# Constant products ahead of the node products at the two ends of a four-layer graph network

## The chip, the cores and the metric

The kernel runs on one core of a Trainium2 chip. The metric is the device time of one launch in microseconds, the median of several runs. A core has five engines that work side by side and each take their own instructions in order: PE (TensorE, matrix products into PSUM), DVE (VectorE), ACT (ScalarE), POOL (GpSimd) and SP (which here issues DMAs). PE has two rows in the profile: PE for the products and PEld for the loads of the stationary operand. TensorE's clock is throttled; the profile reports the share of full speed that was granted.

## The reference

128 graphs of 64 nodes with 128 features pass through four residual layers. `x` is (128, 64, 128), `adj` (128, 64, 64), weighted, about a quarter filled. Cut to what matters:

```python
# layer 0: continuous-filter convolution over all pairs i, j
h = relu(layernorm(x))
Wf = ssp(gauss(adj) @ W1.T + b1) @ W2.T + b2          # (B, N, N, 128)
y = einsum('bjf,bijf->bif', h @ Wa.T, Wf * adj * adj)
x = x + ssp(y @ Wd1.T + bd1) @ Wd2.T + bd2
# layer 1: hyperbolic attention
h = relu(layernorm(x))
p = proj(mobius_add(proj(mobius_matvec(W, h)), proj(expmap0(b_lin))))
loc = clip(logmap(p_i, p_j))                          # all pairs
att = sigmoid(silu(concat(self, loc) @ att_w1.T + att_b1) @ att_w2.T + att_b2)
s = sum_j(att * loc * adj)
s = silu(concat(self, s) @ mlp_w1.T + mlp_b1) @ mlp_w2.T + mlp_b2 + self
x = x + proj(expmap0(silu(logmap0(proj(expmap(s, p))))))
# layer 2: normalised graph convolution
h = relu(layernorm(x));  d = 1 / sqrt(adj.sum(2) + 1e-8)
x = x + (d_i * adj * d_j) @ h @ W + b
# layer 3: message passing
h = relu(layernorm(x));  deg = adj.sum(1)
m = where(deg > 0, (adj.T @ (h @ Ws)) / max(deg, 1) + h @ Wr, 0)
x = x + concat(h, m) @ W_upd
```

## The kernel before

The 128 graphs are cut into 16 groups of 8 (`GROUPS`). Two graphs share the 128 partitions, so a group is four pairs, and a tile of node features is 128 x 4 x 128. Nodes of each graph are sorted by degree, and only the slots of edges that exist are computed: the edge tiles of layers 0 and 1 run over a fixed pattern of slots instead of all pairs. Two constant bf16 tiles belong to that: `slot_k`, the slot numbers, and `bones_b`, a block matrix of ones, one 64 x 64 block for each graph of a pair.

Every stage of a group is a Python generator, a stream, that yields before each step: `load`, `order`, `layer0`, `layer1_nodes`, `layer1_edges`, `rest1`, `rest2`, and smaller streams that they start (`attention`, `rows`, `scores_of`, `heads` and others). The class `Weave` runs these steps in one fixed list, `ORDER`: an entry such as `layer1_nodes@-3` means "one step of that stream for the group three before the current turn". The list is run through once per turn, from turn -6 to turn 21, and groups that don't exist are left out. So in the middle five or six groups at different stages are interleaved on all engines; at the start only the first groups are there, and at the end only the last. The order on PE, DVE, ACT and POOL is exactly the order in which the steps emit instructions; only what stands behind the list (`enough`, the reading of its flag and the branch over a dense fallback) is placed by the scheduler. While a step runs, `w.now` is its stream, with `name` and `group`.

PSUM has two kinds of tiles: `big` (two banks, three buffers) for edge products, and `sm` (one bank, two buffers) for node products. `bank()` hands out the next `sm` bank; PE may write it when whoever read its previous content is done. The steps with a bank that the text speaks of, in their order for one group:

- `layer1_nodes`. It begins with the end of layer 0: the product of `y` with `wd1T` (L1739 to L1743), read by ACT; the product with `wd2T` (L1759), read by DVE. Then the transposes of the normed `h1` (L1243, tile n) read by ACT; the product with `wlinx` (L1794, in a `big`); the transposes of `hh` (L1243); the Gram products (L1932, L1934), read by ACT into `gr`; the product with `attT` (L1250, tile n), which ACT scales into `Sx`.
- `rest1`: the product with `bones` (L2192), read by DVE; after a `big` product (L1264) the hidden layer (L2210, L2211), read by ACT; the product with `m2T` (L1250), read by DVE (L2219).
- `rest2`: after a `big` product (L1264) the one with `w2g` (L1250); the ranks (L2348); the un-sorting product (L1257); the transposes of `h3` (L1243); three products with `wsu`, `wru` and `wupd` on the same transposed tile (L1250); the product with `adj` (L1257). DVE then forms the output (L2402, L2405, four L1307), and SP stores it (L2414).

Lines of helpers appear for whole classes of work: L1243 (`transposes`), L1250 (`pairs_mm`), L1257 (`graphs_mm`), L1264 (`by_graph`), L1217 (`evac`, a copy on ACT). The edge products L2089, L2107, L2111 and L2133 belong to layer 1, L1605, L1627, L1644 and L1673 to layer 0.

Of the kernel before, what the change touches and what calls it, by code (L numbers as in the profile page):

```python
# [11 lines left out]
F32 = mybir.dt.float32  # L12
# [9 lines left out]
GROUPS = B // (2 * NP)  # L22
P = 128
# [747 lines left out]


PE, DVE, ACT, POOL = "PE", "DVE", "ACT", "POOL"
ORDER = """
filter_of00@-2 duo02@-2 rest2@-5 rest2@-5 weights_of20@-2 layer1_nodes@-3 rest2@-5 neighbours00@-2
turned_from2@=0 weights2@=3 turned_from3@=-2 filter_of01@-2 layer1_nodes@-3 filter_of00@-2
# [171 lines left out]
def sparse_stack(ctx: ExitStack, tc: tile.TileContext, ins, out: bass.AP, flag):  # L948
# [10 lines left out]
    psm = ctx.enter_context(tc.tile_pool(name="s_psm", bufs=2, space=PSUM))  # L959

    w = Weave()
    V, S, G, T = nc.vector, nc.scalar, nc.gpsimd, nc.tensor
# [22 lines left out]
    bones_b, tri_b = (const.tile([P, P], BF, name=n) for n in ("bones_b", "tri_b"))  # L985
# [39 lines left out]
    slot_k = const.tile([P, SLOTS + SLOTS % 2], BF, name="slot_k")  # L1025
# [202 lines left out]
    def flat(t):  # L1228
        return t.rearrange("q p n -> q (p n)")

    def bank(n=P):
        return psm.tile([P, 512 // n, n], F32, name="sm", tag="sm")

    def big():
        return pbig.tile([P, 2, 512], F32, name="big", tag="big")
# [3 lines left out]
    def transposes(src):  # L1239

        pt = bank()
        for p in range(NP):
            T.transpose(pt[:, p, :], src[:, p, :], ident)  # L1243
        return pt

    def pairs_mm(lhsT, rhs):

        pt = bank()
        for p in range(NP):
            T.matmul(pt[:, p, :], lhsT=lhsT[:, p, :], rhs=rhs(p), start=True, stop=True)  # L1250
        return pt
# [179 lines left out]
    def order(g, st):  # L1431
# [13 lines left out]
        V.tensor_tensor(own, idb, bl(deg, N), ALU.mult)  # L1445
        yield on(PE, "sm")
        pt = bank(N)
        T.matmul(flat(pt)[:, 0:NP * N], lhsT=bones_b, rhs=flat(last_d), start=True, stop=False)
        T.matmul(flat(pt)[:, 0:NP * N], lhsT=bones_64, rhs=flat(own), start=False, stop=True)
# [971 lines left out]
    with tc.manual_schedule(engines={E.Activation, E.PE, E.DVE, E.Pool}):  # L2421
        for stream in (slots_ranks, weights0, weights1, weights2):
            w.add(stream(), group=-1)
        for g in range(GROUPS):
            st = {}
            for stage in (load, order, layer0, layer1_nodes, layer1_edges, rest1, rest2):
                w.add(stage(g, st), group=g)
        w.run(ORDER, GROUPS)
    assert not w.streams
# [37 lines left out]
```

## Time and profile before

| what | value |
|---|---|
| median of 3 runs | 1784.91 us (1784.58 to 1786.87) |
| the profiled execution | 1786.2 us |
| its span, first to last instruction | 1784.4 us |
| mean granted TensorE clock | 0.941 |
| PE busy | 1580.3 us (89%), 10487 products |
| DVE busy | 1537.2 us (86%) |
| ACT busy | 1507.6 us (84%) |
| POOL busy | 407.2 us (23%) |
| DMA, queue 1 | 52.19 MB, 12.2% of 16 engines |
| chain that ended last | ACT 42%, PE 36%, DVE 13%, issue 4%, POOL 3%, DMA 2% |

All times below are microseconds from the start of the span. The chain that ended last is followed back from the last instruction: at each step to what released it, or to the instruction ahead of it on its engine. "Issue" in it is time in which an engine waited for nothing that the profile shows. In lists of instructions, brackets hold the idle time of the engine ahead of the instruction, and what ended it. Matmuls are pipelined and their ends are modelled, so the length of a group of products includes a tail that overlaps what follows; the distance of starts tells what one costs in a row. An fp32 product of 128 x 512 appears as two records, a bf16 one as one.

### The profile page before, as it was taken

How to read it: one execution, taken by the hardware profiler on the slowest of the kernel's cores; microseconds unless marked ns; L12 is line 12 of the kernel's file. 1: busy time of each engine (PE TensorE's matmuls, PEld its weight loads, DVE VectorE, ACT ScalarE, POOL GpSimd, SP SyncE). 2: the span in 40 equal slices, each digit the busy share in tenths (PEclk: the TensorE clock that was granted, in tenths of full speed). 3: DMA queues.
4: the chain of work that ended last, by engine and by line, in shares of the span. 5: the costliest groups of instructions: out<-in, count | busy, mean ns of one | idle time of the engine just before them, and what ended most of it. 6: DMA issues, size and time to landing. Idle time of an engine off the chain costs nothing.

```text
span 1784.4 us, 30686 instructions
## 1 busy us (share of the span) xinstructions
PE 1580.3 (89%) x10487; PEld 873.9 (49%) x10487; DVE 1537.2 (86%) x4826; ACT 1507.6 (84%) x2816; POOL 407.2 (23%) x701
## 2 busy tenths in 40 slices
PE   3959899998989899898989899898989999897853
PEld 2424444545545455455545454554545555454442
DVE  5559799999999999999999999999999999887843
ACT  2858798989899898989899898989999898986632
POOL 2010113122221413223121312222141322312121
PEclk9989999999999999999999999999999999997875
DMA  2000202011110202011020201111020201102110
GB/s 62 6 1 7 57 7 52 13 38 30 28 46 16 58 7 56 18 34 34 16 58 12 62 7 43 24 27 46 16 58 1 57 11 30 34 15 50 42 29 8
DMA packets 57174, 54.24 MB, mean 30 GB/s; under 512 B 13616, under 2 KB 40624, under 8 KB 57008
## 3 DMA queue, kind: packets, MB, share of 16 engines
q1 hardware_dynamic: 57008, 52.19, 12.2%
q8 instruction: 85, 1.39, 0.3%
q14 instruction: 81, 0.66, 0.1%
HBM read 7.61 MB, written 4.19 MB: 7 GB/s over the span
## 4 chain that ended last, share of the span: by engine, by line
ACT 42%; PE 36%; DVE 13%; issue 4%; POOL 3%; DMA 2%; SPq 1%; DVEq 0%; ACTq 0%
PE big L2107 6%; ACT ex L1634 6%; PE big L1644 5%; PE big L2089 4%; PE sm L1250 4%; ACT ex L1637 4%; ACT ra L1679 4%; PE big L2111 3%; ACT e L1613 3%; ACT e L1610 3%; ACT L923 3%; PE sm L2133 2%; ACT n L1297 2%; ACT ex L2116 2%; ACT va L1594 2%
## 5 line engine op out<-in xcount | busy, mean ns | idle before, releaser
L1644 PE MATMUL big<-ex,w2T 128*128 128x512 f32 (+1 forms) x768 | 300.6, 521 | 12.6 <-ACT ex L1634 5.5
L1649 DVE SCALAR_TENSOR_TENSOR ex<-big,c_L_gnn_b,ra 128x1024 f32<-128x1024 f32 (+1 forms) x160 | 198.4, 1240 | 50.2 <-PE big L1644 49.3
L1627 PE MATMUL big<-e,w1T 64*128 64x512 f32 (+1 forms) x768 | 185.7, 576 | 11.3 <-ACT e L1613 9.1
L1644 PEld LDWEIGHTS big<-ex,w2T 128*128 128x128 f32 x768 | 131.4, 190 | 127.9 <-issue 71.3
L2116 ACT ACTIVATE ex<-big,c_L_gnn_att_b 128x1024 f32<-128x1024 f32 (+1 forms) x160 | 168.0, 1080 | 17.7 <-PE big L2111 17.4
L2107 PE MATMUL big<-va,U 64*128 64x512 f32 (+1 forms) x768 | 175.1, 531 | 7.9 <-DVE va L2092 6.8
L1634 ACT ACTIVATE ex<-big,c_L_gnn_b 128x1024 f32<-128x1024 f32 (+1 forms) x160 | 175.2, 1095 | 3.1 <-PE big L1627 1.6
L1673 PE MATMUL big<-va,a 64*128 64x512 f32 (+1 forms) x768 | 169.7, 540 | 2.2 <-ACT va L1594 1.0
L2111 PE MATMUL big<-slot_r,Sx 64*128 64x512 f32 (+1 forms) x768 | 166.0, 506 | 0.0
L1637 ACT ACTIVATE ex<-ex 128x1024 f32<-128x1024 f32 (+1 forms) x160 | 165.8, 1049 | 0.0
L1679 ACT ACTIVATE ra<-big 128x1024 f32<-128x1024 f32 (+1 forms) x160 | 159.5, 1008 | 5.5 <-PE big L1673 5.5
L1408 DVE TENSOR_TENSOR ex<-ex 128x512 f32<-128x512 f32 (+1 forms) x256 | 141.0, 551 | 1.0
L2072 DVE COPY_PREDICATED att<-oh,th 128x256 f32<-128x256 uint16 x256 | 110.4, 444 | 17.1 <-DMA th<-row 15.7
L2227 POOL TENSOR_TENSOR w<-w,hh 128x512 f32<-128x512 f32 x16 | 22.1, 1383 | 444.5 <-DVE w L2219 431.0
L923 ACT ACT_TABLE_LOAD x92 | 118.0, 1283 | 2.2 <-PEq L2455 0.7
L2089 PE MATMUL big<-oh,pqs 64*64 64x512 bf16 (+1 forms) x1152 | 115.0, 337 | 0.0
L2092 DVE COPY_PREDICATED va<-slot_r,big 128x1024 f32<-128x1024 uint32 (+1 forms) x96 | 103.1, 1075 | 12.9 <-PE big L2089 12.9
L1627 PEld LDWEIGHTS big<-e,w1T 64*128 64x128 f32 x768 | 66.7, 199 | 78.6 <-issue 23.1
L2111 PEld LDWEIGHTS big<-slot_r,Sx 64*128 64x128 f32 x768 | 73.9, 187 | 60.4 <-issue 60.4
L2133 PE MATMUL sm<-ex,aw2b 128*32 128x512 f32 (+1 forms) x640 | 89.3, 589 | 14.4 <-ACT ex L2116 14.4
L1673 PEld LDWEIGHTS big<-va,a 64*128 64x128 f32 x768 | 69.7, 193 | 62.0 <-issue 36.2
L1264 PE MATMUL big<-adjT,v 64*128 64x64 f32 x256 | 30.8, 402 | 71.7 <-ACT v L1292 71.7
(571 smaller groups left out, 3682.0 us busy)
## 6 DMA issues: line engine op xcount, KB each, us to landing
th<-row SPq DMA_DIRECT2D x128, 256.0 KB, 3.5
th<-row SPq DMA_DIRECT2D x64, 104.0 KB, 2.3
x<-in_x_dram SPq DMA_DIRECT2D x16, 256.0 KB, 2.8
out_dram<-v SPq DMA_DIRECT2D x16, 256.0 KB, 2.3
adj<-in_adj_dram SPq DMA_DIRECT2D x16, 128.0 KB, 2.3
e<-in_L_gnn_att_w_dram SPq DMA_DIRECT2D x2, 64.0 KB, 4.3
bR<-in_L_gnn_mlp_w_dram SPq DMA_DIRECT2D x2, 64.0 KB, 3.4
wupd<-in_L_gnn_W_upd_dram SPq DMA_DIRECT2D x1, 128.0 KB, 3.7
```

What stands on the lines that cost most here:

```text
L923: self.scalar.preload_act_table_set({"log": "natural_log_exp_and_others", "silu": "silu_and_others"}[table])
L1627: T.matmul(dst, lhsT=w1T[HALF[h], :], rhs=e[HALF[h], b, 0:W], start=True, stop=True)
L1634: act(ex[:, :, 0:wide], pre[:, :, 0:wide], AF.Exp, bias=b1)
L1637: act(ex[:, :, 0:wide], ex[:, :, 0:wide], AF.Ln, bias=1.0)
L1644: T.matmul(wf[:, b, cols], lhsT=w2T, rhs=ex[:, b if c < 2 else b ^ j, cols], start=True, stop=True)
L1649: V.scalar_tensor_tensor(two.rearrange("q (j r) -> q j r", j=2), wf[:, :, 0:wide], b2s, ra[:, :, 0:wide], ALU.add, ALU.mult)
L1673: T.matmul(nb[:, b, at * W:at * W + W], lhsT=rf[rows, p + j, :], rhs=factors[0][rows, k + j, :], start=True, stop=True)
L1679: act(ra[:, :, 0:wide], nb[:, :, 0:wide], AF.Copy)
L2089: T.matmul(rk[h, k, 0:W], lhsT=pqs[h, s, p, :], rhs=oh[h, p, at:at + W], start=s == 0, stop=s == 2)
L2107: T.matmul(pre[:, b, col], lhsT=U[h, p + k, :], rhs=coefs[h, k, :], start=True, stop=False)
L2111: T.matmul(pre[:, b, col], lhsT=Sx[s][h, p + k, :], rhs=slot_r[h, at:at + W], start=False, stop=s == 1)
L2116: act(a[:, :, 0:wide], pre[:, :, 0:wide], AF.Silu, bias=ab1)
```

## The change

`bank()` learns which stream it works for. If that is `layer1_nodes` of group 0 or of the last group, or `rest1` or `rest2` of the last group, it writes four bf16 products of the constants `bones_b` and `slot_k[:, 0:512]` into the whole new bank ahead of the node product that asked for it. Their results are never read: the node product starts the bank anew. Steps of nested streams (`attention`, `heads`, `order` and the like) have other names and stay as they are, and so do the `big` tiles.

```diff
 PE, DVE, ACT, POOL = "PE", "DVE", "ACT", "POOL"
+KEPT_BUSY = {("layer1_nodes", 0), ("layer1_nodes", GROUPS - 1), ("rest1", GROUPS - 1), ("rest2", GROUPS - 1)}
...
     def bank(n=P):
-        return psm.tile([P, 512 // n, n], F32, name="sm", tag="sm")
+        pt = psm.tile([P, 512 // n, n], F32, name="sm", tag="sm")
+        if w.now and (w.now.name, w.now.group) in KEPT_BUSY:
+            for _ in range(4):
+                T.matmul(flat(pt), lhsT=bones_b, rhs=slot_k[:, 0:512], start=True, stop=True)
+        return pt
```

In the changed kernel's instruction lists this is 92 products and 92 weight loads more on PE, in 23 places: six in `layer1_nodes` of group 0, six in that of group 15, three in `rest1` and eight in `rest2` of group 15. The order on ACT and POOL is the same as before. Behind the hand-written list, the copy of the flag from PSUM (L1566) stands behind the four L1307 of the last group on DVE instead of ahead of them, and SP issues the last store ahead of its load of the flag instead of behind it. Every line of the kernel below the edit is five further down.

## The prediction

> **What bounds the kernel now.** I read the page first: how full the engines are and where the clock drops.
>
> ```profile
> span 1784.4 us, 30686 instructions
> ...
> PE   3959899998989899898989899898989999897853
> ...
> PEclk9989999999999999999999999999999999997875
> ```
>
> In the middle PE, DVE and ACT all stand at nine tenths and the TensorE clock (PEclk) is nearly full. Only at the two ends, where one group is alone, do both sag: mean clock 0.941. Next I took the chain of waits near the last group's node chain, because a product that is put into PE's queue costs time only where PE is on that chain.
>
> ```profile
> 1603.81 1.41 PE big L2089 x12
> 1605.22 1.05 PE sm L1739 x2
> 1606.28 0.86 PE sm L1740 x2
> ...
> 1612.97 0.86 PE big L2107 x4
> 1613.83 0.46 PE big L2111 x4
> 1614.29 1.98 PE sm L1759 x16
> 1616.27 1.00 PE sm L2133 x8
> ...
> 1623.67 0.21 PE big L2111 x4
> 1623.88 0.60 PE sm L1243 x4
> 1624.51 0.59 ACT n L1217
> ```
>
> Columns: start, length, engine, tile, line, count. From 1599 to 1619 the chain is PE alone, each piece starting where the last ends: whatever is inserted here moves the end. Then the timeline of PE in rest2 of the last group, whose brackets give the idle time ahead of each product:
>
> ```profile
> 1754.65 1.97 PE L1264 MATMUL big<-adjT,v 64*128 64x64 f32 x16 [22.43 <-ACT v L1292]
> 1757.31 2.08 PE L1250 MATMUL sm<-w2g,a 128*128 128x128 f32 x8 [0.68 <-ACT a L1217]
> 1761.01 0.39 PE L2348 MATMUL sm<-r,bones_b 128*128 128x256 bf16 x1 [1.62 <-DVE r L2345]
> 1761.98 1.97 PE L1257 MATMUL sm<-v,r 64*64 64x128 f32 x16 [0.58 <-DVE r L2350]
> 1768.05 1.63 PE L1243 MATMUL sm<-ident,v 128*128 128x128 f32 x4 [4.09 <-ACT v L1292]
> 1770.35 2.07 PE L1250 MATMUL sm<-wsu,a 128*128 128x128 f32 x8 [0.68 <-ACT a L1217]
> 1772.21 1.91 PE L1250 MATMUL sm<-wru,a 128*128 128x128 f32 x8
> ```
>
> Four constant products fit free of charge only into brackets longer than themselves. Last, the clock itself. In microsecond windows it changes at 1704.9, 1718.5, 1722.0, 1728.8, 1735.7, 1776.5: steps of a multiple of 3.41 us. So I cut the tail on that grid (length, PE busy, others, clock, DMA):
>
> ```profile
> 1718.40:1721.80 3.40, 1.31 (x4) 0.55 (x4) 0.41 (x3) 2.67 (x6) 1.02 (x1) 0.99 0.01 2
> 1756.00:1759.40 3.40, 2.71 (x14) 2.22 (x14) 0.00 (x0) 0.59 (x1) 1.11 (x1) 0.50 0.00 0
> 1769.60:1773.00 3.40, 2.73 (x13) 2.65 (x13) 0.00 (x0) 1.13 (x2) 0.00 (x0) 0.50 0.00 0
> 1773.00:1776.50 3.50, 3.50 (x22) 3.27 (x22) 0.57 (x1) 1.19 (x5) 0.00 (x0) 0.50 0.00 0
> ```
>
> 2.7 of 3.4 us busy did not lift the half clock (it stays 0.50 after 1759.4); 3.5 of 3.5 did (1.00 from 1776.5). A slice at full clock with 1.31 busy lost it. Over the whole trace, full clock survived slices down to 47% busy.
>
> **The change, priced.** It removes and moves nothing in the emitted order ahead of the last lines; it adds 23 bursts of four bf16 128x512 products with a weight load each: 6 in layer1_nodes of group 0, 6 + 3 + 8 in layer1_nodes, rest1 and rest2 of group 15. The profile has no such row. At full clock: twelve L2089 products (64-row halves, in pairs, with their own weight loads) take 1.41 us, so 0.235 for 512 columns and 0.94 for four; L1448 and L1449 (256 columns) start 0.11 apart, so 0.88. I take **0.9**. At half clock: 24 records of L1250 take 5.49 (0.229 each) against 16 of L1759 in 1.98 (0.124), a ratio of 1.85: 1.67, or twice 0.9: 1.8. I take **1.75**. A burst waits for its bank alone, as its product did before, so it starts when PE is done with what is ahead; what is queued behind it is all later PE work.
>
> Group 0. At L1739, PE comes straight from L1250 (99.81 for 2.07) and ACT waits for the result (L1747 at 105.36): +0.9 (1.75 if it all falls in the half clock before 104). At L1759 (idle 1.30 before), at L1243 of n (4.62) and of hh (1.66) the idle time swallows it: 0; without that cover each would cost 0.9. At L1932 there is no gap, ACT's copy of gr starts 0.17 after PE and DVE has 0.25 to spare: +0.7 (0 to 0.9). At the attT product at 163.38, DVE's next eviction L1649 starts 0.76 after PE is done: +0.2 (0 to 0.9). Together 1.8. Since the chain runs on without a break, I let this shift last to the end.
>
> Group 15, layer1_nodes. L1739, L1759 and L1243 of n stand in the PE stretch shown: 3 x 0.9 = 2.7 (2.6 to 2.8). L1243 of hh follows L1264 (1647.27 for 2.08) with no gap, and ACT's copy at 1650.41 is next on the chain; half clock until about there: +1.3 (0.9 to 1.75). L1932, idle 0.68 before: 0.9 - 0.68 = +0.2 (to 1.07). The attT product at 1666.79 follows wupd without gap; DVE's L2040 has 0.1 to spare: +0.8 (to 0.9). Sum 5.0.
>
> rest1. At L2192 (idle 3.01) nothing; uncovered it would be 1.75. At L2210, straight after wupd: 0.9, less 0.4 because L2210 and L2211, 2.15 on the chain (half clock until 1728.8), would then run whole at full clock: the L2210/L2211 of the group before start 0.86 apart, so 1.72. Net +0.5 (0.2 to 1.3). At m2T (idle 0.17 before) 0.9 - 0.17 = +0.75, as DVE's L2219 waits for it. Sum 1.25.
>
> rest2, where the clock could pay back. Ahead of w2g: 1.75 cold against 0.68 idle, +1.07. But L1264, this burst, w2g and the next burst are now 7.5 us without a gap, so a whole slice fills, and the clock rises inside w2g: -0.5. Burst two (0.9) fits into 1.62; L2348 saves 0.1; burst three costs 0.9 - 0.58 = +0.3; L1257 goes from 1.97 to the 1.09 of its row at 1730.05: -0.9. Burst four fits into 4.09, transposes save 0.15 (1.63 to 1.48, their row at 1720.32). They fill 1.3 of a slice as at 1718.4, so the clock falls again: burst five 1.75 - 0.68 = +1.07. Bursts six to eight have no gap: 3 x 0.9 = +2.7; by then a slice is full, one earlier than before, so wru and wupd save 0.85 each (8 x 0.229 against 8 x 0.124), -1.7, and the adj product 0.3. Sum **+1.5**. Where the slices fall is open: shifting the grid through one period moves the sum between +0.4 and +2.7.
>
> A rule speaks on the fall. The Trainium skill, "TensorE: Matmul & The Clock Gate", Part 1, has the clock halved after an idle window of about 3.4 us. This trace halves it after slices 38% to 47% busy. By the page the clock would hold through the transposes and this part would be about -1.0, the total 1791.6; I go by the slices.
>
> Last lines: the flag's copy (L1566) moves behind the four L1307, and the branches that close the program wait for it; the final output DMA is issued ahead of SP's flag load instead of behind it. 1.1 us later on that path, of which SP's own path (DMA at 1778.77, branch 1779.20) hides most: +0.3 (0 to 0.5). Clock gained elsewhere, as n's transposes in group 0 (1.08 to 0.66) and wsu of group 14: -0.6 (0 to -1.8).
>
> Sum: 1.8 + 5.0 + 1.25 + 1.5 + 0.3 - 0.6 = 9.25. The profiled execution took 1786.2 (span 1784.4 and 1.8 around it) and would take 1795.5; it lies 1.3 above the median 1784.91, so the median should be **1794**. All lower ends together give +5, all upper ones +15.
>
> **Rivals.** *The clock is held up.* Bursts at half clock count for more than my slices say and keep the tail warm from 1645 on. For: the clock rose at 1718.5 on a slice not quite full. Against: 80% busy was not enough in four slices. Price: on the chain in half-clock stretches lie L1257 and L1264 of 1645 (4.0), L1243 and wsu to wupd of 1659 (7.1), L1257 of 1714 (2.0), wsu to L2210 of 1722 (6.8) and rest2 (15.0). At full clock by the rows above (1.09 for each L1257 and L1264, 0.124 a record for the rest) these 34.9 are 20.4: 14.5 back. The bursts, all warm, cost 11.8: net -2.7, 1782.2, not slower. It decides once more than 11.8 is won back; the bursts stand near only half of those stretches.
>
> *The shift is absorbed.* Bursts in the full stretches (group 0 and the first three of group 15, 4.5) vanish in pieces that the chain calls "issue" (2.23 at 103.12, 0.64 at 1627.68) and in the th DMA landings; hh, L1932 and attT too (2.3). Left: 2.45, 1787.4. Against: around 1605 PE idles nowhere.
>
> *The clock gets worse.* Bursts shift the work so that slices stay unfilled: against the sum, rest2 2.7 for 1.5 (+1.2), the burst of L1739 in group 0 cold (+0.85), hh and L1932 cold (+1.3), L2210 at its upper end (+0.8), attT cold (+0.85), no gain elsewhere (+0.6): 9.25 + 5.6 = 14.85, 1799.8. For: each burst then outlasts its bracket. Against: a gapless run longer than 6.8 us always holds a whole slice.
>
> **How the numbers follow.** Forecast 0.72, absorbed 0.12, worse 0.08, held up 0.08. The range 1788 to 1798 holds most of the forecast's own spread (1790 to 1800 with every end at once) and reaches down to the absorbed case; what it leaves out is the held-up case, most of the worse one and part of the absorbed. Less than 0.2% (3.6 us) can't be told from no change. Faster needs the held-up case with still less paid for bursts: half of it, 0.04. Within: the other half and most of the absorbed, 0.14. Slower: 0.82.
>
> **What would show it.** On the chain, new L1236-type pieces of 0.9 before L1739, L1759 and n's L1243 of group 15; idle brackets gone before wsu and w2g; full clock from about 1760 to 1770 (shifted) in rest2, half again at wsu. PE busy rises by about 20 us. I am wrong if the chain jumps over the bursts near 1605, or if the clock in rest2 stays full after the transposes.

## The result, and the profile after

| | kernel before | changed kernel |
|---|---|---|
| median (lowest to highest, runs) | 1784.91 us (1784.58 to 1786.87, 5) | 1793.49 us (1793.09 to 1795.09, 5) |
| ratio of the times, 95% interval | | 1.0045 [1.0034, 1.0055] |
| profiled execution: span | 1784.4 us | 1793.0 us |
| mean granted TensorE clock | 0.941 | 0.947 |

The change costs 8.6 us. A median of 1794 had been forecast, in a range of 1788 to 1798. A second set of its runs, taken beside three of the experiments, gave 1795.20 (1.0057 [1.0043, 1.0071]).

The page of the changed kernel:

```profile
span 1793.0 us, 30869 instructions
...
PE 1597.6 (89%) x10579; PEld 879.5 (49%) x10579; DVE 1538.0 (86%) x4826; ACT 1507.5 (84%) x2816; POOL 405.2 (23%) x701
...
PE   3969899998989899998989899898989899896854
...
PEclk9989999999999999999999999999999999998876
```

PE is busy 17.3 us more. The mean clock of this pair rose by 0.006, and in the page only its last four digits moved (7875 before, 8876 now). Over all runs it is 0.940 to 0.947 for the changed kernel and 0.937 to 0.945 for the unchanged one, so little changed. The constant products did not hold the clock up: between 1600 and 1780 half clock lasted 92.3 us before and 78.5 us now (81.7 in a second profile of the changed kernel).

The chain of waits at the same place as before (start, length, engine, tile, line, count; all lines are five further down, and L1236 is the burst):

```profile
1605.41 1.41 PE big L2094 x12
1606.83 0.97 PE sm L1236 x4
1607.80 0.86 PE sm L1744 x2
1608.65 0.86 PE sm L1745 x2
...
1616.65 0.97 PE sm L1236 x4
1617.62 1.78 PE sm L1764 x16
...
1627.01 0.97 PE sm L1236 x4
1627.98 0.45 PE sm L1248 x4
```

Each burst is a piece of the chain, as forecast. But a burst adds less than its 0.97: the product behind it is shorter than it was (0.86 for 1.05, 1.78 for 1.98, 0.45 for 0.60). So 0.15 to 0.2 us that belonged to that product alone now lies inside the burst; why, the traces do not show. The starts of what follows moved by 0.77, 0.76 and 0.82.

The same stretch of rest2 of the last group, on PE's timeline (brackets: idle time ahead, and what ended it):

```profile
1760.53 1.97 PE L1269 MATMUL big<-adjT,v 64*128 64x64 f32 x16 [22.44 <-ACT v L1297]
1762.43 1.89 PE L1236 MATMUL sm<-slot_k,bones_b 128*128 128x512 bf16 x4
1764.11 1.92 PE L1255 MATMUL sm<-w2g,a 128*128 128x128 f32 x8
1765.82 1.17 PE L1236 MATMUL sm<-slot_k,bones_b 128*128 128x512 bf16 x4
1767.65 0.27 PE L2353 MATMUL sm<-r,bones_b 128*128 128x256 bf16 x1 [0.66 <-DVE r L2350]
...
1768.71 1.09 PE L1262 MATMUL sm<-v,r 64*64 64x128 f32 x16
...
1773.90 1.63 PE L1248 MATMUL sm<-ident,v 128*128 128x128 f32 x4 [3.13 <-ACT v L1297]
1775.32 1.91 PE L1236 MATMUL sm<-slot_k,bones_b 128*128 128x512 bf16 x4
1777.03 1.92 PE L1255 MATMUL sm<-wsu,a 128*128 128x128 f32 x8
```

The brackets before w2g and wsu are gone, as forecast. The un-sorting product (L1262, L1257 before) takes 1.09 instead of 1.97, as it would at full clock; the transposes' bracket shrank from 4.09 to 3.13. Cut on the clock's steps (length, busy time of PE, PE's weight loads, DVE, ACT and POOL with counts, granted clock, DMA):

```profile
1759.30:1762.70 3.40, 2.17 (x17) 1.92 (x18) 0.16 (x1) 1.80 (x5) 1.36 (x3) 0.50 0.00 0
1762.70:1766.10 3.40, 3.40 (x13) 2.44 (x12) 0.00 (x0) 0.43 (x1) 0.28 (x1) 0.50 0.00 0
1766.10:1769.50 3.40, 2.74 (x23) 1.47 (x23) 1.94 (x6) 0.00 (x0) 0.00 (x0) 1.00 0.00 0
1769.50:1772.90 3.40, 1.27 (x10) 0.37 (x6) 1.62 (x12) 0.59 (x1) 1.06 (x2) 1.00 0.00 0
1772.90:1776.40 3.50, 2.50 (x7) 1.21 (x8) 0.16 (x1) 2.23 (x5) 0.16 (x1) 0.50 0.00 0
1776.40:1779.80 3.40, 3.40 (x13) 2.43 (x12) 0.00 (x0) 0.59 (x1) 0.00 (x0) 0.51 0.00 0
```

The full slice from 1762.7 lifted the clock at 1766.1, when the product with w2g had just ended. The slice with 1.27 busy dropped it again at 1772.9, so the transposes at 1773.90 already ran at half clock (1.63, as before). The next full slice, from 1776.4, lifted it once more at 1779.8.

Where the 8.6 us lie can be read from how much later the same instruction starts than before. The table sets the prediction's terms beside two profiled executions of the changed kernel; the second is that of e12_whole_again, below.

| term | forecast | first profile | second profile |
|---|---|---|---|
| what group 0 leaves (at 1603.7) | 1.8 | 1.60 | 1.31 |
| layer1_nodes of group 15 (to L2192) | 5.0 | 3.27 | 3.82 |
| rest1 (to m2T) | 1.25 | 1.09 | 1.08 |
| rest2 (to the first output operation) | 1.5 | 1.27 | 1.37 |
| last lines (to the end of the span) | 0.3 | 1.4 | 1.7 |
| clock gained elsewhere | -0.6 | in the rows above | in the rows above |
| sum | 9.25 | 8.6 | 9.2 |

The first row can't be put down to group 0: the profiles of seven kernels below without a burst there (e2, e3, e5, e6, e8, e9 and e10) stand at -2.05 to +1.72 us at the same place, from one execution to the next. And the rows of rest2 and of the last lines share a gain. With the flag's copy behind them, the output operations no longer stand behind it, and the first of them starts 1.14 us after the start of the last node product, the one with adj; with the copy ahead it is 1.52 to 1.69 (all at full clock). Without this, the row of rest2 would be about 0.4 to 0.55 higher, and that of the last lines as much lower.

### The profile page after: what moved, and what is told of

Same layout as the page of the kernel before. It is cut to its first block, busy times and chain, and to the rows that moved or that the text cites. A ratio compares the mean times of both kernels' runs of the same rounds, so it can differ in the third digit from the quotient of the medians.

```text
span 1793.0 us, 30869 instructions
## 1 busy us (share of the span) xinstructions
PE 1597.6 (89%) x10579; PEld 879.5 (49%) x10579; DVE 1538.0 (86%) x4826; ACT 1507.5 (84%) x2816; POOL 405.2 (23%) x701
## 4 chain that ended last, share of the span: by engine, by line
ACT 44%; PE 36%; DVE 11%; issue 4%; POOL 3%; DMA 1%; SPq 1%; DVEq 0%; ACTq 0%
PE big L2112 6%; ACT ex L1639 6%; PE big L1649 4%; PE big L2094 4%; ACT ex L1642 4%; ACT ra L1684 4%; PE sm L1255 4%; ACT e L1618 3%; PE big L2116 3%; ACT L924 3%; ACT e L1615 3%; PE sm L2138 2%; ACT ex L2121 2%; ACT n L1302 2%; ACT va L1599 2%
## 6 DMA issues: line engine op xcount, KB each, us to landing
th<-row SPq DMA_DIRECT2D x64, 104.0 KB, 2.3
```

## The experiments

Each kernel's time is compared with runs of the unchanged kernel on the same chip. Besides the ratio, the difference of the means is given, with a 95% interval from resampling the runs; single runs of one kernel lie up to 5 us apart, so about 1 us is the least that five to eleven runs can tell.

**The change in three parts.** The edit is the set of streams alone:

```diff
-KEPT_BUSY = {("layer1_nodes", 0), ("layer1_nodes", GROUPS - 1), ("rest1", GROUPS - 1), ("rest2", GROUPS - 1)}
+KEPT_BUSY = {("layer1_nodes", 0)}                               # e1_start
+KEPT_BUSY = {("layer1_nodes", GROUPS - 1)}                      # e2_nodes15
+KEPT_BUSY = {("rest1", GROUPS - 1), ("rest2", GROUPS - 1)}      # e3_rests15
```

> Only the six bursts in layer1_nodes of group 0 are left. Theory (a shift set early lasts to the end, since the chain of waits has no break): +1.45 us, the shift that the changed kernel's trace shows from 180 us on. Rival (the full middle of the kernel absorbs it in its short idle pieces): within 0.5 us of the kernel before.

> Only the six bursts in layer1_nodes of group 15. Theory (bursts in the PE-full stretch and behind it cost their own length where PE has no gap): 3 x 0.8 for L1739, L1759 and the transposes of n, 0.5 for hh and the Gram product, 0.35 for attT: +3.2 us. The prediction's terms were 2.7 + 1.5 + 0.8 = +5.0. Rival (absorbed in DMA landings and pieces called issue): under +1 us.

> Only the eleven bursts in rest1 and rest2 of group 15; the flag's copy stands behind the four output operations on DVE as in the changed kernel. Theory: rest1 +1.1, rest2 +1.35, the flag and the branches behind it +1.4: +3.85 us, with the clock rising inside the product with w2g and falling again after the transposes. Rival (the bursts hold the clock up and pay back): at most +1 us. Where the slices of 3.41 us fall is open: 1 us either way.

| kernel | median (runs) | ratio | difference of means |
|---|---|---|---|
| e1_start | 1785.17 (11) | 1.0002 [0.9993, 1.0011] | +0.3 [-0.5, 1.2] |
| e2_nodes15 | 1788.93 (11) | 1.0025 [1.0015, 1.0034] | +3.9 [3.2, 4.7] |
| e3_rests15 | 1789.07 (7) | 1.0022 [1.0011, 1.0033] | +3.5 [2.1, 4.9] |

The parts add up to 7.7 us. The whole is 8.7 by its means in the first set of runs and 10.2 in the second. With an interval of 0.8 to 1.4 us either way on each part, that shows no effect between them, and doesn't rule out one of 1 to 2 us. The node chain of group 15 costs less than the 5.0 of the prediction. The start alone costs nothing that could be told, though its trace shows a shift of 1.25 us at 200 us and 0.61 at 1603.7; in that profile the rest of the shift melted at the clock's edges in the tail (0.20 left at 1667.9, 0.03 at 1754.7), which came 0.3 us earlier than in the profile before while the work came later.

**Bursts in places that should be covered.** Counts per bank take the place of the set; here three places in layer1_nodes of group 0 (L1764, n, hh), the first bank of rest1 and banks two and four of rest2 have their four products, and no others:

```diff
+BURSTS = {("layer1_nodes", 0): (0, 4, 4, 4, 0, 0), ("rest1", GROUPS - 1): (4, 0, 0),
+          ("rest2", GROUPS - 1): (0, 4, 0, 4, 0, 0, 0, 0)}
...
+    calls = {}
...
-        if w.now and (w.now.name, w.now.group) in KEPT_BUSY:
-            for _ in range(4):
+        if w.now:
+            key = w.now.name, w.now.group
+            calls[key] = calls.get(key, -1) + 1
+            for _ in range(dict(enumerate(BURSTS.get(key, ()))).get(calls[key], 0)):
```

> Seven bursts alone, those that stand in idle brackets longer than 1.2 us: the product with wd2T and the transposes of n and of hh in group 0; the product with bones in rest1, and the ranks, the un-sorting product being left out, and the transposes of h3 in rest2 of group 15 (six places in all: three, one, two). Theory (a covered burst costs nothing): 0 us, down to -0.5 if the transposes of n stay at full clock. Rival (any burst delays what follows it on PE, covered or not, by 0.1 to 0.9): +0.6 to +5 us.

Measured: 1785.75 (11 runs), ratio 1.0000 [0.9991, 1.0009], difference +0.4 [-0.3, 1.1]. Six of the 23 bursts are free within about a microsecond. One of them is not covered as the prediction read it: at the product with wd2T of group 0 the burst itself waits for 1.29 us, as the product did, and starts only behind that idle time. What takes up its 0.86 us is a second idle piece, of 0.83 us, that the kernel before has inside that product.

**Does an early shift last?** e1_start left two answers: a shift from group 0 is given back on the way, or it was only too small to be seen. One long burst at L1744 of group 0 settles that:

```diff
+BURSTS = {("layer1_nodes", 0): (24,)}
```

> One burst of 24 products ahead of L1739 in group 0, nothing else: some 6.4 us of PE time, of which about 5 us are left behind L1743. Theory of the prediction (an early shift lasts to the end): +4.5 to +5.5 us. Rival A (a fixed slack of about 1 us in the middle takes it up, as six bursts of four brought +0.3 instead of +1.45): +3.5 to +4.5. Rival B (each rise of the clock at its fixed slice edge halves a shift, so little of any shift is left after fifteen groups): under +2 us.

Measured: 1791.29 (5 runs), 1.0042 [1.0029, 1.0056], +7.3 [6.4, 8.3]. In the trace the shift is 5.2 us behind the burst, 5.3 to 6.1 through the middle and 5.3 at 1754. A shift of 5 us set early lasts. The time rose by more than the trace's shift and by more than any theory had said; the profiled execution (span +4.5) is the fastest of its kernel, and the rest stays unexplained.

**The last burst and the flag's copy.** In the changed kernel the flag's copy stands behind the four output operations. e5 and e11 take the last burst out, which puts the copy ahead again; e10 adds one single product to the unchanged kernel, which puts it behind; e12 is the whole change once more, beside e10 and e11.

```diff
+BURSTS = {("rest1", GROUPS - 1): (4,) * 3, ("rest2", GROUPS - 1): (4,) * 7}    # e5_rests15_no_last
+BURSTS = {("rest2", GROUPS - 1): (0, 0, 0, 0, 0, 0, 0, 1)}                     # e10_last_one
+BURSTS = {("layer1_nodes", 0): (4,) * 6, ("layer1_nodes", GROUPS - 1): (4,) * 6,    # e11_all_but_last
+          ("rest1", GROUPS - 1): (4,) * 3, ("rest2", GROUPS - 1): (4,) * 7}
```

> As the kernel with the bursts of rest1 and rest2 alone, without the last burst (ahead of the product with adj); with it gone the flag's copy stands ahead of the four output operations again, as in the kernel before. Theory (the flag behind the output costs 1.4 us at the end, the burst 0.86): 2.2 us less than that kernel, +1.3 against the kernel before; the last output operation to the end of the span shrinks from 8.2 us (first output operation at 1784.85, end at 1793.0) to 6.8. Rival (the flag's place is hidden behind SP's own path): 0.9 to 1.2 us less.

> The unchanged kernel with one single constant product, ahead of the very last node product (the one with adj in rest2 of the last group). That is enough to put the flag's copy behind the four output operations and SP's last store ahead of its load of the flag, as in the changed kernel. The product itself costs 0.23 us. Theory from the traces so far (first output operation to the end of the span 6.6 to 7.0 us with the copy ahead, 7.7 and 8.2 behind): 0.9 to 1.4 for the order, +1.1 to +1.6 in all, and 7.7 us or more from the first output operation to the end. Prediction's term (SP's own path hides most of it, +0.3, at most 0.5): +0.5 in all, 7.3 us at most.

> The changed kernel without its last burst (ahead of the product with adj in rest2): 22 bursts, and the flag's copy is ahead of the output operations again. Against the whole change run beside it: theory, 0.9 for the burst and 0.9 to 1.4 for the order of the last lines, -1.8 to -2.3 us; prediction's terms, 0.9 + 0.3 = -1.2 us. The order of the last lines shows in the trace as 6.6 to 7.0 us from the first output operation to the end instead of 8.2.

> The whole change once more, on the same chip as the three others, to be compared with the one without the last burst: 8 to 9.3 us more than the unchanged kernel, by both theories.

| kernel | median (runs) | ratio | difference of means |
|---|---|---|---|
| e5_rests15_no_last | 1788.45 (7) | 1.0021 [1.0009, 1.0032] | +3.6 [2.0, 5.1] |
| e10_last_one | 1786.29 (11) | 1.0007 [0.9998, 1.0016] | +1.2 [0.3, 2.1] |
| e11_all_but_last | 1792.35 (5) | 1.0041 [1.0027, 1.0055] | +7.4 [6.7, 8.0] |
| e12_whole_again | 1795.20 (5) | 1.0057 [1.0043, 1.0071] | +10.2 [9.2, 11.1] |

e5 missed: against e3 nothing was saved, with runs of each that spread over 5 us. The better pair is e11 against e12, on one chip and with a spread under 3 us: -2.8 [-3.5, -2.0], where the prediction's terms gave -1.2. Not all of it is the order of the last lines: the two profiled executions end 2.9 us apart, and 0.9 of that is there ahead of the last burst, where their instructions are the same. The burst is 1.1 more, and 0.9 lies behind the start of the last node product. The end of the timeline of e10, one product more than the unchanged kernel:

```profile
1776.94 0.38 PE L1574 MATMUL sm<-over,ones 128*128 128x1 f32 x2
1777.16 1.13 DVE L1316 SCALAR_TENSOR_TENSOR v<-sm,rdeg,v 128x128 f32<-128x128 f32 x4
1778.20 0.15 DVE L1575 CAST flag<-sm 128x1 int32<-128x1 f32 x1
1778.31 0.38 SPq L2423 DMA_DIRECT2D out_dram<-v  x1
```

and of e11, the change without its last burst:

```profile
1783.61 0.15 DVE L1576 CAST flag<-sm 128x1 int32<-128x1 f32 x1
1783.73 1.13 DVE L1317 SCALAR_TENSOR_TENSOR v<-sm,rdeg,v 128x128 f32<-128x128 f32 x4
1784.89 0.38 SPq L2424 DMA_DIRECT2D out_dram<-v  x1
```

The store is issued 1.15 us after the first output operation in both. What differs is when the engines read the flag and branch, SP last, from the trace's records of the sequencers, counted from the start of the first output operation:

| | copy ahead (10 profiles) | copy behind (4 profiles) |
|---|---|---|
| flag's copy starts | -0.12 to -0.08 | 1.04 |
| SP issues the last store | 1.14 to 1.15 | 1.15 to 1.16 |
| SP's branch | 1.58 to 1.60 | 2.46 |
| SP's next instruction after that branch | 3.11 to 3.48 later | 3.33 to 4.06 later |
| end of the span | 6.62 to 6.99 | 7.72 to 8.45 |

With the copy ahead, SP loads the flag while DVE still works on the output; behind it, the load comes after the store. The branch then stands 0.87 us later, in every profile. The rest of the 1 to 1.5 us is in how long SP is away at the branch, which also differs between executions. DVE, ACT and POOL branch 1.1 us later too (DVE at 1.85 instead of 0.69 to 0.74), but SP is the last to go on in all 14 profiles. Since the first output operation comes sooner with the copy behind, the net price is smaller: from the start of the last node product to the end of the span it is 8.15 to 8.68 us with the copy ahead (seven profiles) and 8.86 to 9.59 with it behind (three, all at full clock), on the mean 0.9 us.

**Can products of that kind hold the clock?** The change's bursts have one size everywhere: too long for the brackets on the chain, too short for the gaps in which the clock falls. In these three kernels the counts are made to the brackets of the trace, and a stretch of idle PE ahead of a by-graph product is filled in its own `big` bank:

```diff
+BURSTS = {("rest2", GROUPS - 1): (2, 5, 2, 16, 2)}                    # e6_warm_rest2
+BIG = {("rest2", GROUPS - 1): 90}                                     # e6_warm_rest2
+BURSTS = {("rest2", GROUPS - 3): (5, 10, 5, 22, 2), ("rest1", GROUPS - 2): (9,),    # e8, e9
+          ("layer1_nodes", GROUPS - 1): (0, 0, 0, 0, 2), ("rest2", GROUPS - 2): (2, 4, 1, 7, 2),
+          ("rest1", GROUPS - 1): (11,), ("rest2", GROUPS - 1): (2, 5, 2, 16, 2)}
+BIG = {("rest2", GROUPS - 3): 3, ("rest2", GROUPS - 2): 9, ("rest2", GROUPS - 1): 90}    # e8_warm_tail; 102 for 90 in e9_warm_102
...
     def by_graph(lhsT, rhs):
...
+        for _ in range(BIG.get((w.now.name, w.now.group), 0)):
+            T.matmul(pt[:, 0, :], lhsT=bones_b, rhs=slot_k[:, 0:512], start=True, stop=True)
```

> Constant products in rest2 of group 15 alone, sized to the idle time: 90 into the big tile ahead of the first product (PE is idle for 22.4 us there), then 2, 5, 2, 16 and 2 ahead of the first five node products, none ahead of the last three, which have no gap. Theory (each 3.41 us slice stays over half busy, so the clock stays full and all products of rest2 run at full clock): -5.4 us, from L1264 -0.6, w2g -0.9, L2348 -0.1, L1257 -0.9, the transposes -0.15, wsu to wupd -2.5, adj -0.3. Rival (the constants don't hold the clock, or overfill their gaps): 0 to +2 us.

> As the kernel with sized products in rest2 of group 15, and also in the idle brackets of rest2 of groups 13 and 14, rest1 of groups 14 and 15 and the Gram product of group 15. Theory (the half-clock stretches of the tail go, none of the products stands where PE has no gap): L1257 and L1264 at 1645 -2.0, transposes and wsu to wupd at 1659 -2.7, L1257 at 1714 -0.9, wsu to L2210 at 1722 -2.9, rest2 of group 15 -5.4: -11 to -14 us. Rival (brackets overfilled, or the chain moves to another engine): -5 us or less gain.

> The kernel with sized products, with 102 instead of 90 in the long idle stretch of the last group's rest2. With 90, PE stood idle for 3.02 us ahead of the by-graph product and the clock was half from 1749.0 to 1755.8; twelve more at 0.218 us each fill 2.6 of the 3.02. Theory (a slice must stay full for the clock to stay): the clock is full at the by-graph product and at w2g, these go from 1.97 and 2.00 to 1.1 each, the 2 and 5 products between them fit into their brackets, so 2 to 3 us less than with 90: a ratio to the unchanged kernel of about 0.995. Rival (the filling was long enough, or it now delays the by-graph product): within 0.5 us of the kernel with 90.

| kernel | median (runs) | ratio | difference of means |
|---|---|---|---|
| e6_warm_rest2 | 1780.96 (11) | 0.9985 [0.9976, 0.9994] | -2.8 [-3.8, -1.8] |
| e8_warm_tail | 1777.68 (5) | 0.9963 [0.9950, 0.9977] | -6.6 [-7.8, -5.3] |
| e9_warm_102 | 1774.54 (5) | 0.9943 [0.9929, 0.9957] | -9.8 [-10.9, -8.6] |

e6 and e8 gave half of what was expected, and the windows of e6 (same columns) show one reason: the 90 products were done too soon.

```profile
1745.00:1748.40 3.40, 3.40 (x17) 1.57 (x16) 0.85 (x5) 1.23 (x9) 2.14 (x4) 1.00 0.00 0
1748.40:1751.80 3.40, 1.31 (x7) 0.39 (x4) 1.88 (x12) 0.00 (x0) 1.52 (x4) 1.00 0.00 0
1751.80:1755.20 3.40, 2.50 (x18) 1.92 (x18) 0.16 (x1) 2.13 (x5) 1.38 (x2) 0.50 0.00 0
```

One slice with 1.31 busy, and the by-graph product meets half clock. Twelve products more (e9) close the gap. The windows below lie on e8's steps; on e9's own, PE is busy 3.35 of 3.4 us from 1746.5 and 2.84 from 1749.9:

```profile
1749.00:1752.40 3.40, 2.94 (x23) 1.61 (x21) 0.16 (x1) 1.91 (x5) 1.37 (x3) 1.00 0.00 0
1752.40:1755.80 3.40, 2.71 (x17) 1.67 (x16) 1.46 (x5) 0.32 (x1) 0.54 (x1) 1.00 0.00 0
```

and on PE's timeline of e9 the products run at full clock, w2g and wsu in 1.16 where the kernel before had 2.08 and 2.07, the by-graph product in 1.59 for 1.97:

```profile
1728.12 21.96 PE L1275 MATMUL big<-slot_k,bones_b 128*128 128x512 bf16 x99
1750.50 1.59 PE L1278 MATMUL big<-adjT,v 64*128 64x64 f32 x16 [0.41 <-ACT v L1306]
...
1752.78 1.16 PE L1262 MATMUL sm<-w2g,a 128*128 128x128 f32 x8
...
1763.74 1.16 PE L1262 MATMUL sm<-wsu,a 128*128 128x128 f32 x8 [0.24 <-ACT a L1221]
```

In e9 the clock is full from 1541.7 to 1770.4 us without a break. It is the fastest of all: against e8 on another chip -2.6 [-4.1, -1.2], the 2 to 3 us that were expected of the twelve products, and 19 us below the changed kernel's first median.

## Why the prediction was right

The forecast's mechanism held: where PE is on the chain a burst adds most of its length, in the covered places it adds nothing that can be told, and in rest2 the clock rises, falls and rises again. That the sum (9.25) came within 0.65 us of the profile is partly luck: the node chain was put 1.2 to 1.7 us too high, the last lines too low, and inside rest2 several steps missed and cancelled.

- **Node chain of group 15, forecast 5.0, measured 3.3 and 3.8 in the traces and 3.9 [3.2, 4.7] by e2_nodes15.** All three bursts of the PE stretch are on the chain, and "3 x 0.9 = 2.7" was 2.35, because each takes over 0.15 to 0.2 us of the product behind it. The step that failed most is the Gram product at L1932, where the prediction put "0.9 - 0.68 = +0.2": -0.35 was measured in both profiles. It left out what the burst ahead of hh does to the transposes behind it, shown in the timeline of the kernel before and then of the changed one:

```profile
1649.31 1.07 PE L1243 MATMUL sm<-ident,hh 128*128 128x128 f32 x4
1651.05 0.69 PE L1932 MATMUL sm<-n 128*64 128x64 f32 x16 [0.68 <-ACT n L1217]
```

```profile
1653.22 1.13 PE L1236 MATMUL sm<-slot_k,bones_b 128*128 128x512 bf16 x4
1654.19 0.60 PE L1248 MATMUL sm<-ident,hh 128*128 128x128 f32 x4
1654.63 1.03 PE L1236 MATMUL sm<-slot_k,bones_b 128*128 128x512 bf16 x4
1655.59 0.69 PE L1937 MATMUL sm<-n 128*64 128x64 f32 x16
```

  The clock rises at 1650.2 before, inside the transposes, and at 1653.5 in the changed kernel, where the burst has pushed the transposes past that edge: they take 0.60 instead of 1.07 and give back what the Gram burst costs. The hh burst itself cost +0.94 in this profile and +1.32 in the second, for +1.3 in the forecast; the attT burst +0.35 and +0.49 for +0.8.
- **Last lines, forecast 0.3 (at most 0.5), measured 1.4 and 1.7 from the first output operation, about 0.9 net of its earlier start.** "SP's own path hides most of it" is wrong: that path got longer too. SP's load of the flag and its branch follow the store in series, 0.87 us later. The profile of e10_last_one shows it with a single product, and its time, +1.2 [0.3, 2.1] with 0.23 for the product, agrees; e5 against e3 showed nothing.
- **Group 0, forecast 1.8 to the end, and "clock gained elsewhere", -0.6.** From ahead of the first burst (99.8) to 200 us the work falls 1.45 us behind in the first profile of the changed kernel and 1.49 in that of e1_start: 0.8 at L1739, -0.5 where the transposes of n run more at full clock (counted under "elsewhere"), 1.0 at the Gram product, 0.2 at attT. It is 1.2 in e11_all_but_last and 2.9 in the second profile, whose clock edges lie elsewhere. So locally the two terms fit in three profiles of four. That a large shift lasts to the end, e7_start_long shows. Alone the part cost +0.3 [-0.5, 1.2], which leaves out 1.8 and not the 1.2 that the two terms leave. How much of it is paid within the whole change stays open, as the drift at 1603.7 is larger.
- **rest1, 1.25 for 1.1. rest2, 1.5 for 1.3 to 1.4.** In rest2 the steps fit less well than the sum. The clock did not rise "inside w2g" but as it ended, and that part gained 0.16 us instead of 0.5. It fell a slice earlier than forecast: not on the transposes but on the slice ahead of them, with the end of the un-sorting product and burst four. So the transposes did not get shorter (1.63, not 1.48). Burst six still began at half clock and cost 1.2 instead of 0.9. Against that, the output operations came 0.7 us sooner behind the last node product, where 0.3 was put, in part because the flag's copy was gone from ahead of them.
- **Covered places, forecast 0:** +0.4 [-0.3, 1.1] for six of them.
- **The rule weighed against the trace.** The Trainium skill, "TensorE: Matmul & The Clock Gate", Part 1, speaks of an idle window of about 3.4 us. Here slices that were still 1.27, 1.31 and 0.97 us busy (changed kernel, e6, e8) lost the clock, so the slices were the better guide. The 1791.6 us worked out by the page lies below all ten runs of the changed kernel, but with other terms over a microsecond off that total alone wouldn't decide. Nor is the busy share of a slice a sharp rule. Slices with 1.94 of 3.4 us busy (changed kernel, 1633.0), 2.27 (e4, 1630.2) and 2.23 (e8, 1656.9) lost the clock too, though others kept it at 47%. And the prediction's "3.5 of 3.5 did" lift it doesn't always hold: in the kernel before, PE was busy for all of the slice from 517.0 at half clock, and only the next one lifted it.
- **Rivals.** "The clock is held up" fell for this change: half clock only went from 92.3 to 78.5 us. Its mechanism is real, as e9 shows, but needs products sized to their brackets. "The shift is absorbed" (1787.4) fell by 6 us, "the clock gets worse" (1799.8) by the clock, of which the tail lost none.

## What to carry to other kernels

Filler products won time here only where they fitted into the idle brackets and kept the 3.41-us slices well filled (2.6 us and more of each from 1736 to 1767 in e9). The same product, four ahead of each of 23 node products, cost 8.6 us, and sized by the trace's brackets it won 9.8. Read a filler's price on the chain, less what the product behind it gets shorter (0.15 to 0.2 us here). And look at what an edit does to the last few lines of a program: one product there moved a flag's copy behind the output and cost about a microsecond, for the branch that ends the program waits for it.

## What the runs showed of the hardware

The clock's steps keep a grid of 3.41 us of their own, whose place against the program differs from run to run. The profiles of two kernels with the same instructions up to there show it at the start: before, half clock 93.7 to 104.0 and 114.2 to 121.0; in e9, which adds nothing to group 0, half also from 108.1 to 111.5 and from 114.9 to 128.6. Its work was 0.23 us late at 101.7 and 1.92 us late at 109.8, and still 1.72 at 1603.7. That profiled execution, at 1776.98, is the slowest of the five of e9. The grid's place may be a source of the up to 5 us between runs of one kernel, but it was not tried by itself.

A full slice need not be work on data: in e9 one constant product, 102 times in a row in 21.96 us (99 of them recorded), held the clock while DVE, ACT and POOL worked beside it.

The branch that closes the program holds SP for 3.1 to 4.1 us, in all 14 profiles.
